# A ternary feed-forward split by batch, with keys loaded whole, in a gated cross-attention network

## The chip, the cores and the metric

One core of a Trainium2 chip runs the kernel. The metric is the device time of one execution in microseconds (us), the median of several runs. The engines are PE (matrix products; PEld is its weight load, which overlaps), DVE (vector), ACT (activation functions and copies), POOL and SP (which issues most DMAs). Each takes its instructions in order.

## The reference

Input x is 2 x 512 x 256 (1,024 tokens, 8 blocks of 128, four per batch), the context 2 x 1024 x 256. Four layers follow one another, each x = x + tanh(g) * attention(x, context) and then x = x + tanh(g) * ffn(norm(x)), with norms inside:

- layer 0: attention at sampled positions; an int8 feed-forward
- layer 1: attention with 16 heads of 8; a mixture of 8 experts (MoE), one expert per token, 192 tokens per expert at most
- layer 2: attention with 16 heads of 16; the ternary feed-forward
- layer 3: attention with 8 heads of 4; a channel-mixing feed-forward

The ternary feed-forward, with all weights in {-1, 0, 1} and a scale per output column, is

```
a  = silu((h @ w1) * s1) * ((h @ w2) * s2)     # 256 -> 1024, gated
b  = gelu((a @ h1) * t1)                       # 1024 -> 1024
c  = gelu((b @ h2) * t2)                       # 1024 -> 1024
y  = (c @ w3) * s3                             # 1024 -> 256
```

for every token by itself, so the two batches are independent in it. Softmax attention here subtracts the largest score of each row and head before the exponential.

## The kernel before

**Order of work.** The kernel is one program written layer by layer; a tile framework takes its instructions, gives them buffers by tags with a fixed number of slots, and orders the instructions of each engine by their dependences and slots. `keep_in_program_order` pins an instruction where it was written.

**Attention** (`attention`, from line 1042) works on the two batches in turn. `queries(b)` transposes the normalised blocks of batch b and multiplies with the query weights (L1070, L1076) into QT. Then, per block and group of heads, the scores of 128 queries are made (L1143, into `scores` or a bank) and their largest values reduced on DVE (L1150, L1152), which ends in qa. In the main part the scores are made again transposed (L1174), ACT takes the exponential (L1179), PE multiplies with the values (L1186). The first 20 largest-score steps, the lead, run before the first exponential; `queries(1)` goes beside them. What the layer in front still has to do is handed in as `before`: a function of a range of blocks that gives a generator of steps. It is called for batch 0's blocks ahead of everything; for batch 1's blocks its steps alternate with those of `queries(0)`, and what is left of them runs before the lead.

**Keys and values** of all attentions are computed at the start and kept in DRAM. K is stored per head in HD + 1 rows of 2,048 columns. `loaded_keys` (L1011 to L1026) makes one tile for four heads, each in a quarter of the 128 partitions: POOL sets the tile to zero (L1019), then one DMA per head brings its rows (L1021): 17 rows of 8 KB in layer 2, 5 in layer 3.

**MoE.** Each expert's products end in `ye`, stored to DRAM `yg`; its last part, `rest` (L1424 to L1438), gathers each block's rows with an indirect DMA on POOL (L1427) and adds them to x on DVE (L1434). It is the `before` of attention 2. The norm's statistics, square root (L161, ACT), reciprocal (L162, DVE) and offsets (L168) follow, and ACT makes h (L184).

**Ternary feed-forward** (`ternary_ffn`, from L1582). An fp32 activation is split in three bf16 parts (`split`, L1605 to L1608: two casts on ACT, two subtractions on DVE), each multiplied with the upper 16 bits of the weights, which are exact for ternary values. `upper` also reduces the lower 16 bits of every weight (L1596) into `low`. The norm of all eight blocks comes first, then the first layer over all 1,024 tokens; the second and third layer (`gelu_layer`) load a 512 KB slice of weights per 128 output columns (L1662, two slots) and multiply it with 1,024 tokens (L1634, 48 matmuls of 512 columns per slice). Then a matmul sums `low` (`psl`, L1683), `more` is read as a flag (L1685), and every engine branches over `any_weights` (L1689), a fallback for weights that are not ternary, which doesn't run with these inputs. w3T, attention 3's keys and values are loaded ahead of the flag. The last product (L1696) with the update of x (L1701, L217) is attention 3's `before`: eight blocks of 16 matmuls.

**The zeros** in DRAM that the MoE needs are written by `prepare_routing` beside attention 1, from a tile `zero`.

Of the kernel before, what the change touches and what calls it, by code (L numbers as in the profile page):

```python
# [8 lines left out]

# [70 lines left out]
class _Net:  # L80
# [829 lines left out]
    def prepare_context(self):  # L910
        nc = self.nc
        self.kd, self.vd = {}, {}
        for name, H, HD in (("l1", 16, 8), ("l2", 16, 16), ("l3", 8, 4)):
            k = self.dram.tile([H, HD + 1, B * M], F32, name=f"K_{name}")
            self.kd[name] = k
            nc.sync.dma_start(
                k[:, HD, :].rearrange("h (c m) -> h c m", m=P),
                _bc(self.ones[:H].unsqueeze(1), [H, B * M // P, P]),
            )
# [93 lines left out]
    def loaded_keys(self, name, H, HD):  # L1013
# [3 lines left out]
        for g in range(H // 4):  # L1017
            k = self.wide("KT")([P, B, M])
            nc.gpsimd.memset(k, 0.0)  # L1019
            for h in range(4):  # L1020
                nc.sync.dma_start(  # L1021
                    k[32 * h : 32 * h + HD + 1].rearrange("r b m -> r (b m)"),
                    self.kd[name][4 * g + h],
                )
            KT.append(k)
        return KT  # L1026

    def loaded_values(self, name, H):
        V = []
        for b in range(B):  # L1030
            v = self.big.tile([P, M // P, H * 32], F32, tag=f"v{b}", name=f"V{b}")
            self.nc.sync.dma_start(
                v, self.vd[name][ts(b, M)].rearrange("(j p) c -> p j c", p=P)
            )
            V.append(v)
        return V

    def attention(
        self, name, KT, V, H, HD, scale, gate, before, bq=None, bv=None, bo=None, aside=None
    ):  # L1040

# [50 lines left out]
        for _ in first:  # L1092
            next(second, None)
        for _ in second:
            pass
        second = queries(1)
# [149 lines left out]
        for k, _ in enumerate(up_to(LEAD, True)):  # L1246
            run_later()
            if k % 2:
# [51 lines left out]
    def moe_ffn(self, gate):  # L1300
# [121 lines left out]
        KT = self.loaded_keys("l2", 16, 16)  # L1422

        def rest(blocks, bank):  # L1424
            y = self.big.tile([P, BPB, D], F32, tag="e", name="yn", bufs=4)
            for k, n in enumerate(blocks):
# [5 lines left out]
                )  # L1432
            for k, n in enumerate(blocks):
                nc.vector.scalar_tensor_tensor(  # L1434
                    self.x[:, n, :], y[:, k, :], some[:, n : n + 1], self.x[:, n, :],
                    ALU.mult, ALU.add,
# [79 lines left out]
    def prepare_routing(self):  # L1516
# [6 lines left out]
        for to, k in ((self.xg[: NE * CAP], NE * CAP // P), (self.yg[NE * CAP :], T // P)):  # L1523
            nc.sync.dma_start(
                to.rearrange("(k p) f -> p k f", p=P), _bc(zero.unsqueeze(1), [P, k, D])
            )
        self.rank, self.first, self.behind = (
# [54 lines left out]
    def ternary_ffn(self, gate, loads):  # L1582
# [9 lines left out]
        def upper(w):  # L1592
# [6 lines left out]
            )  # L1599
            return w.bitcast(BF16).rearrange("p c (n two) -> p c n two", two=2)[:, :, :, 1]  # L1600
# [9 lines left out]
        hT = self.norm_transposed()  # L1610
        parts = self.big.tile([P, 3, DC, T], BF16, tag="v1", name="hTs")
        for n2 in range(NB // 2):
            at = ts(n2, 2 * P)
            r = self.big.tile([P, DC, 2 * P], F32, tag="avj", name="rest", bufs=2)
            split(hT[:, :, at], [parts[:, i, :, at] for i in range(3)], r)

        def stored(tags, name):

            tiles = []
            for i, part in enumerate(tags):  # L1620
                tiles.append([])
                for k, (tag, bufs, n) in enumerate(part):
                    t = self.big.tile([P, n, T], BF16, tag=tag, name=f"{name}{i}{k}", bufs=bufs)
                    tiles[-1] += [t[:, c] for c in range(n)]
            return lambda i, c, at: tiles[i][c][:, at]

        e2 = [("e", 4, HC // 2)] * 2
        h1 = stored((e2, e2, [("q", 1, HC)]), "hid1")

        def product(ps, w, oc, src, chunks):  # L1630
            for c in range(chunks):
                for i in range(3):
                    for t in range(2):
                        nc.tensor.matmul(  # L1634
                            ps[:, ts(t, 512)], lhsT=w[:, c, ts(oc, P)], rhs=src(i, c, ts_(t, 512)),
                            start=(c == 0 and i == 0), stop=(c == chunks - 1 and i == 2),
                        )

        def keep(dst, oc, at, make):
            g = self.big.tile([P, 512], F32, tag="avT", name="g", bufs=2)  # L1640
            make(g)
            r = self.big.tile([P, 512], F32, tag="avj", name="rest", bufs=2)
            split(g, [dst(i, oc, at) for i in range(3)], r)

        w1, w2 = upper(w12[:, 0]), upper(w12[:, 1])
        for oc in range(HC):
            pa = self.pss.tile([P, T], F32, tag="sc", name="pa")
            pb = self.pss.tile([P, T], F32, tag="sc", name="pb")
            for ps, w in ((pa, w1), (pb, w2)):
                product(ps, w, oc, lambda i, c, at: parts[:, i, c, at], DC)  # L1650
            si = self.wide("si")([P, T])
            nc.scalar.activation(si, pa, AF.Silu, scale=self.col("w1s")[:, oc : oc + 1])
            for t in range(2):
                at = ts_(t, 512)
                keep(h1, oc, at, lambda g: nc.vector.scalar_tensor_tensor(
                    g, pb[:, at], self.col("w2s")[:, oc : oc + 1], si[:, at], ALU.mult, ALU.mult,
                ))

        def gelu_layer(name, scale, src, done):
# [269 lines left out]
```

## Time and profile before

| what | us |
|---|---|
| median of 3 runs | 1298.85 (1297.12 to 1301.19) |
| profiled execution | 1298.23 |
| its span | 1296.5 |
| PE busy | 1156.7 (89%) |
| DVE busy | 720.3 (56%) |
| ACT busy | 607.5 (47%) |
| POOL busy | 228.3 (18%) |
| mean granted TensorE clock | 0.933 |

The span runs from the first to the last instruction; the execution's time is 1.7 us longer. Busy shares are means over stages with different limits, so the stages are to be looked at one by one. In order of time: the MoE's last product ends near 562, attention 2 has its first transposes at 587.3, its last product with the values near 844, the ternary first layer begins at 862.55 and ends at 909.3, the two wide layers end at 1075.3, the last product begins at 1084.1, attention 3's first exponential is at 1149.2, and the end is at 1296.5. In a timeline's line stand: start, duration, engine, line, operation, output<-inputs, shapes, count, and in brackets how long the engine had been idle and what ended it.

### The profile page before, as it was taken

The numbers are of one execution on the slowest core, as the hardware profiler recorded it, in microseconds if no ns is written. First come the engines' busy times: TensorE is split into PE (matmuls) and PEld (weight loads), VectorE is DVE, ScalarE is ACT, GpSimd is POOL, SyncE is SP. The second block draws the span as 40 slices with busy tenths as digits, with TensorE's granted clock in tenths as the row PEclk, the third lists the DMA queues.
The fourth block names the chain that finished last, engine by engine and source line by source line (L and its number), as shares of the span: only waits on it lengthen the run. The fifth ranks groups of instructions, "written<-read, shape, count | busy, mean of one in ns | idle before, by whom it ended". The sixth has DMA issues, their size and how long they took to land. (4 is left out here: it accounts for less than half of the span.)

```text
span 1296.5 us, 16857 instructions
## 1 busy us (share of the span) xinstructions
PE 1156.7 (89%) x6576; PEld 540.6 (42%) x6596; DVE 720.3 (56%) x1106; ACT 607.5 (47%) x1166; POOL 228.3 (18%) x204
## 2 busy tenths in 40 slices
PE   6987499999998989937999899969999997999977
PEld 3334333333334578823333233334444445543324
DVE  5794678787764111114788778448333111588635
ACT  2422236888874311103488678646333110258761
POOL 1043201334320200131033233000000000113200
PEclk9978698999999989977899999979999998989988
DMA  6033530000211345420000100000122112000000
GB/s 220 1 118 111 116 137 5 1 1 1 66 34 41 111 155 190 156 68 27 16 2 1 66 1 2 17 18 1 34 84 58 58 33 80 9 1 1 10 0 33
DMA packets 56837, 67.49 MB, mean 52 GB/s; under 512 B 4064, under 2 KB 45568, under 8 KB 56288
## 3 DMA queue, kind: packets, MB, share of 16 engines
q1 hardware_dynamic: 52856, 61.07, 15.0%
q0 software_dynamic: 896, 2.49, 0.7%
q10 hardware_dynamic: 2992, 2.70, 0.6%
q8 instruction: 57, 0.93, 0.3%
q14 instruction: 36, 0.29, 0.1%
HBM read 49.93 MB, written 16.32 MB: 51 GB/s over the span
## 5 line engine op out<-in xcount | busy, mean ns | idle before, releaser
L1152 DVE TENSOR_REDUCE part<-scores 128x2 f32<-128x1024 f32 x290 | 341.8, 1219 | 92.5 <-PE bank L1174 77.1
L1179 ACT ACTIVATE e<-bank 128x512 f32<-128x512 f32 x580 | 302.2, 601 | 121.1 <-PE bank L1174 89.4
L1174 PE MATMUL bank<-qa,KT 32*128 32x512 f32 x1160 | 306.1, 634 | 0.6 <-DVE o L1213 0.6
L1143 PE MATMUL scores<-KT,QT 32*128 32x512 f32 x1160 | 293.9, 641 | 4.2 <-DVE part L1152 4.2
L1198 POOL TENSOR_TENSOR avT<-avT,avj 128x512 f32<-128x512 f32 x113 | 143.2, 1268 | 345.9 <-ACT avj L1197 345.9
L1186 PE MATMUL bank<-e,V 128*32 128x512 f32 x1280 | 182.8, 607 | 2.5 <-ACT e L1179 2.5
L1143 PEld LDWEIGHTS scores<-KT,QT 32*128 32x128 f32 x1160 | 100.6, 190 | 157.3 <-DVE part L1152 115.3
L1634 PE MATMUL pg<-hid,wg_h 128*128 128x512 bf16 x752 | 165.1, 379 | 0.8
L1174 PEld LDWEIGHTS bank<-qa,KT 32*128 32x128 f32 x1160 | 117.2, 188 | 36.0 <-issue 18.2
L1634 PEld LDWEIGHTS <-wg_h 128*128 128x128 bf16 x768 | 75.1, 98 | 90.6
L1019 POOL MEMSET KT<- 128x2048 f32 x10 | 18.0, 1821 | 375.9 <-PE pg L1634 157.3
L1186 PEld LDWEIGHTS bank<-e,V 128*32 128x32 f32 x1280 | 28.3, 108 | 106.2 <-ACT e L1179 94.9
L1197 ACT COPY avj<-bank 128x512 f32<-128x512 f32 x113 | 69.2, 612 | 6.7 <-PE bank L1186 6.7
L1402 PE MATMUL py<-w2e,h 128*96 128x256 f32 x256 | 57.4, 379 | 0.0
L1596 DVE TENSOR_REDUCE low<-wg_h 128x1 f32<-128x1024 uint16 x16 | 19.5, 1217 | 57.1 <-DMA wg_h<-in_h2T 54.4
L1606 DVE TENSOR_TENSOR rest<-g,hid 128x512 f32<-128x512 f32 x32 | 21.2, 690 | 51.5 <-ACT hid L1605 51.3
L1070 PE MATMUL bank<-ident,h 128*128 128x128 f32 x48 | 11.7, 369 | 39.0 <-ACT h L184 32.2
L1402 PEld LDWEIGHTS py<-w2e,h 128*96 128x96 f32 x256 | 41.2, 163 | 12.2
L1386 PE MATMUL ph<-xeT,w1e 128*128 128x192 f32 x256 | 45.1, 337 | 0.0
L1386 PEld LDWEIGHTS ph<-xeT,w1e 128*128 128x128 f32 x256 | 43.6, 198 | 1.3 <-DVE xeT L109 0.6
L1076 PE MATMUL bank<-hT,w_l_wq 128*128 128x512 f32 x80 | 41.4, 644 | 2.1 <-DVE part L1150 1.4
L1667 ACT ACTIVATE hid<-pg,cols 128x512 f32<-128x512 f32 x16 | 10.1, 683 | 70.2 <-PE pg L1634 70.2
(303 smaller groups left out, 1325.2 us busy)
## 6 DMA issues: line engine op xcount, KB each, us to landing
w1e<-in_W SPq DMA_DIRECT2D x8, 1024.0 KB
w2e<-in_W SPq DMA_DIRECT2D x8, 1024.0 KB
V_l<-v1st SPq DMA_DIRECT2D x16, 256.0 KB
V<-V_l SPq DMA_DIRECT2D x2, 2048.0 KB
wg_h<-in_h1T SPq DMA_DIRECT2D x8, 512.0 KB
wg_h<-in_h2T SPq DMA_DIRECT2D x8, 512.0 KB
K_l<-kst SPq DMA_DIRECT2D x12, 256.0 KB
KT<-K_l SPq DMA_DIRECT2D x16, 136.0 KB
```

The source lines that it names most:

```text
L1076: nc.tensor.matmul(ps, lhsT=wq[:, dc, ts(c, P)], rhs=hT[:, dc, ts(b, S)], start=(dc == 0), stop=(dc == DC - 1),)
L1143: nc.tensor.matmul(sc[i], lhsT=QT[r : r + 32, g, (b * BPB + k) * P : (b * BPB + k + 1) * P], rhs=KT[g][r : r + 32, b, ts(half, 512)], star ...
L1152: nc.vector.tensor_reduce(to, both, AX.X, ALU.max, negate=True)
L1174: nc.tensor.matmul(t, lhsT=KT[g][r : r + 32, b, ts(j, P)], rhs=augmented[n][r : r + 32, :], start=True, stop=True,)
L1179: nc.scalar.activation(e[:, h, :], t, AF.Exp, scale=scale)
L1186: nc.tensor.matmul(po[32 * h : 32 * h + 32, :], lhsT=V[b][:, j, ts(4 * g + h, 32)], rhs=e[:, h, :], start=True, stop=True,)
L1197: nc.scalar.copy(t, po)
L1198: nc.gpsimd.tensor_tensor(part["oT"], part["oT"], t, ALU.add)
L1386: nc.tensor.matmul(ps[:, k // 2, k % 2, :CAP], lhsT=w1[:, dc, ts(4 * fp + k, P)], rhs=xeT[:, dc, :], start=(dc == 0), stop=(dc == DC - 1),)
L1402: nc.tensor.matmul(ps, lhsT=h1[:, fc, ts(t, HCAP)], rhs=w2[:, fc, :], start=(fc == 0), stop=(fc == HC - 1),)
L1606: nc.vector.tensor_tensor(r, g, hi, ALU.subtract)
L1634: nc.tensor.matmul(ps[:, ts(t, 512)], lhsT=w[:, c, ts(oc, P)], rhs=src(i, c, ts_(t, 512)), start=(c == 0 and i == 0), stop=(c == chunks - ...
```

## The change

1. K of layers 2 and 3 has 32 rows per head in DRAM. `prepare_routing` fills the unused rows with zeros, with three more DMAs on SP. `loaded_keys` brings a tile of four heads with one DMA of 128 rows of 8 KB (1 MB): four for layer 2, two for layer 3, with no memset. Layer 1 is as before.
2. In the MoE's `rest` the x updates of batch 1 are kept in program order.
3. The ternary feed-forward is computed batch by batch. Batch 0 is normalised first, its first layer begins, batch 1's norm goes beside it, then batch 1's first layer. Batch 0 goes through the second and third layer, with the check of the weights' lower bits (`note`) in that pass. Then come the flag and the branch, and only after them the loads of w3T, the keys, and the weights of the second layer again. Batch 0's last product (four blocks) lies beside the first four steps of batch 1's second layer. Batch 1's third layer and last product become attention 3's `before`.
4. `attention` has a new argument, `late`, set for attention 3 alone: `queries(0)` runs by itself, and every one of the 20 lead steps is followed by one step of a chain of batch 1's third layer (8 steps), its last product (4 steps) and `queries(1)`.
5. The gate of the feed-forward's update is now `own`: the gate, or zero where the fallback ran; the fallback does its own last product.

The core of the diff:

```diff
@@ attention K in DRAM
-            k = self.dram.tile([H, HD + 1, B * M], F32, name=f"K_{name}")
+            rows = HD + 1 if name == "l1" else 32
+            k = self.dram.tile([H, rows, B * M], F32, name=f"K_{name}")
...
@@ loaded_keys
-            nc.gpsimd.memset(k, 0.0)
-            for h in range(4):
-                nc.sync.dma_start(
-                    k[32 * h : 32 * h + HD + 1].rearrange("r b m -> r (b m)"),
-                    self.kd[name][4 * g + h],
-                )
+            kd = self.kd[name][4 * g : 4 * g + 4]
+            flat = k.rearrange("p b m -> p (b m)")
+            if kd.shape[1] == 32:
+                nc.sync.dma_start(flat, kd.rearrange("h r m -> (h r) m"))
+            else:
+                nc.gpsimd.memset(k, 0.0)
+                for h in range(4):
+                    nc.sync.dma_start(flat[32 * h : 32 * h + kd.shape[1]], kd[h])
...
@@ attention
         first, second = queries(0), before(range(BPB, NB), bank)
         for _ in first:
-            next(second, None)
-        for _ in second:
-            pass
-        second = queries(1)
+            if not late:
+                next(second, None)
+        if late:
+            second = chain(second, queries(1))
+        else:
+            for _ in second:
+                pass
+            second = queries(1)
...
         for k, _ in enumerate(up_to(LEAD, True)):
             run_later()
-            if k % 2:
+            if k % 2 or late:
                 next(second, None)
...
@@ MoE rest
+            stay = self.tc.keep_in_program_order if blocks.start else lambda i: i
             for k, n in enumerate(blocks):
-                nc.vector.scalar_tensor_tensor(
-                    self.x[:, n, :], y[:, k, :], some[:, n : n + 1], self.x[:, n, :],
-                    ALU.mult, ALU.add,
+                stay(
+                    nc.vector.scalar_tensor_tensor(
+                        self.x[:, n, :], y[:, k, :], some[:, n : n + 1], self.x[:, n, :],
+                        ALU.mult, ALU.add,
+                    )
                 )
...
@@ prepare_routing
+        for name, HD in (("l2", 16), ("l3", 4)):
+            for h in range(0, self.kd[name].shape[0], 8):
+                to = self.kd[name][h : h + 8, HD + 1 :, :]
+                nc.sync.dma_start(
+                    to.rearrange("h r m -> h (r m)").rearrange("h (c m) -> h c m", m=D),
+                    _bc(zero[:8].unsqueeze(1), [8, (31 - HD) * B * M // D, D]),
+                )
...
@@ ternary_ffn
+        def first_layer(b, dst):
+            for oc in range(HC):
+                ps = self.pss.tile([P, 2, S], F32, tag="sc", name="pab")
+                for k in range(2):
+                    product(ps[:, k], upper(w12[:, k]), oc, [parts[:, b, i] for i in range(3)], DC)
+                si = self.wide("si")([P, S])
+                nc.scalar.activation(
+                    si, ps[:, 0], AF.Silu, scale=self.col("w1s")[:, oc : oc + 1]
+                )
+                keep(dst, oc, lambda g: nc.vector.scalar_tensor_tensor(
+                    g, ps[:, 1], self.col("w2s")[:, oc : oc + 1], si, ALU.mult, ALU.mult
                 ))
+                yield
+        def layer(b, name, scale, src, done):
             for oc in range(HC):
                 w = self.big.tile([P, HC, P], F32, tag="o4", name="wg_h", bufs=2)
                 nc.sync.dma_start(w, d[name][:, ts(oc, P)].rearrange("(c p) n -> p c n", p=P))
+                if b == 0:
+                    note(w)
+                ps = self.pss.tile([P, S], F32, tag="sc", name="pg")
                 product(ps, upper(w), 0, src, HC)
+                done(oc, lambda g: nc.scalar.activation(
+                    g, ps, AF.Gelu, scale=self.col(scale)[:, oc : oc + 1]
+                ))
+                yield
...
+        normed(0)
+        note(w12[:, 0])
+        note(w12[:, 1])
...
+        steps = first_layer(0, h1[0])
+        for _ in range(2):
+            next(steps)
+        normed(1)
+        all_of(steps)
...
+        all_of(first_layer(1, h1[1]))
...
+        all_of(layer(0, "h1T", "h1s", h1[0], lambda oc, make: keep(to, oc, make)))
...
+        h3, steps = third(0, to)
+        all_of(steps)
...
-        w3 = self.weight("w3T", HID, D, self.big, "wide", bufs=4)
-        loaded = loads()
         flag = nc.values_load(more[0:1, 0:1], min_val=0, max_val=1)
         with self.tc.If(flag != 0):
-            self.any_weights(hT, h3)
+            self.any_weights(gate, hT)
+
+        w3 = self.weight("w3T", HID, D, self.big, "wide", bufs=4)
+        KT = keys()
+        V = [values(0)]
...
+        to1 = h2()
+        for oc, _ in enumerate(
+            layer(1, "h1T", "h1s", h1[1], lambda oc, make: keep(to1, oc, make))
+        ):
+            if oc < BPB:
+                last(h3, oc, self.ps1.tile([P, D], F32, tag="one", name="pw3"))
+        h31, steps1 = third(1, to1)
         def rest(blocks, bank):
+            if blocks.start == 0:
+                return
+            yield from steps1
+            V.append(values(1))
             for n in blocks:
-                ps = bank(D)
...
+                last(h31, n, bank(D))
                 yield
```

## The prediction

> **What bounds the kernel now.** I read the page's first two parts (share of each engine, the span in slices), then a table of busy time by stretches cut at the stages' borders, then the timeline at those borders, and last the transfers by tile. PE is the engine that ends things: 1156.7 of 1296.5 us. What can be won therefore lies where it stands still or runs at a low clock. The stretches (length; busy us of PE, PEld, DVE, ACT, POOL; granted clock; DMA share; GB/s):
>
> ```profile
> 562.00:587.30 25.30, 0.00 (x0) 0.00 (x0) 7.92 (x29) 2.13 (x4) 9.50 (x9) 0.60 0.21 68
> 862.50:868.00 5.50, 3.18 (x7) 1.01 (x8) 4.73 (x8) 3.54 (x7) 0.00 (x0) 0.50 0.00 0
> 868.00:909.30 41.30, 41.14 (x183) 18.34 (x184) 29.03 (x43) 25.43 (x37) 0.00 (x0) 0.96 0.00 1
> 909.30:1075.30 166.00, 165.16 (x755) 75.43 (x769) 41.84 (x54) 40.71 (x67) 3.61 (x2) 1.00 0.18 53
> 1075.30:1084.00 8.70, 0.09 (x1) 0.00 (x1) 0.16 (x1) 2.55 (x3) 0.00 (x0) 0.73 0.90 243
> 1084.00:1090.30 6.30, 6.21 (x17) 5.00 (x18) 0.00 (x0) 0.00 (x0) 0.00 (x0) 0.56 0.17 49
> 1090.30:1117.00 26.70, 26.70 (x125) 22.74 (x124) 11.14 (x31) 4.24 (x8) 0.00 (x0) 1.00 0.00 1
> 1119.00:1149.20 30.20, 26.74 (x113) 11.92 (x117) 25.69 (x37) 6.71 (x12) 5.62 (x3) 0.80 0.02 6
> ```
>
> Row 1: 25.3 us without a matmul between the MoE layer and attention 2. Rows 2 and 3: the ternary first layer starts in gaps. Row 4: its two 1024-wide layers leave PE no gap, and DVE is idle three quarters of the time. Row 5: at the flag PE stands for 8.7 us, with the DMA engines 0.90 busy. Row 6: the first block of the last product at half clock. Row 8: attention 3's lead (20 largest-score steps before its first exponential) holds DVE for 25.69 of 30.2 us. So: DVE is idle beside PE's longest stretch, and PE then waits for DVE.
>
> **Keys as whole loads, and the pinned updates.** Inside row 1 (start, us, idle before and releaser):
>
> ```profile
> 569.92 1.05 POOL L1427 DMA_INDIRECT yn<-yg,gt  x1 [6.07 <-DMA KT<-K_l]
> 575.67 0.48 DVE L1434 SCALAR_TENSOR_TENSOR x<-yn,gt,x 128x256 f32<-128x256 f32 x1 [13.23 <-DMA yn<-yg,gt]
> ...
> 582.52 0.20 ACT L161 ACTIVATE rs<-rs 128x4 f32<-128x4 f32 x1 [18.42 <-DVE rs L160]
> 583.53 0.48 DVE L1434 SCALAR_TENSOR_TENSOR x<-yn,gt,x 128x256 f32<-128x256 f32 x1 [1.05 <-DMA yn<-yg,gt]
> 584.81 0.48 DVE L1434 SCALAR_TENSOR_TENSOR x<-yn,gt,x 128x256 f32<-128x256 f32 x1 [0.79 <-DMA yn<-yg,gt]
> ...
> 586.26 0.16 DVE L162 RECIPROCAL rs<-rs 128x4 f32<-128x4 f32 x1
> ...
> 587.30 0.29 PEld L1070 LDWEIGHTS bank<-ident,h 128*128 128x128 f32 x2 [25.75 <-ACT h L184]
> ```
>
> The 16 loads of 17 rows move 26 to 28 GB/s at a DMA share of 0.06, one engine of 16; the gathers, behind the last memset (562.05 to 563.85), begin at 569.92. In the change four loads of 1 MB take the place of 16 of 136 KB, and at the 214 to 347 GB/s that the 512 KB weight loads show they are over in 3 to 5 us each, before or while the last product runs. The gathers wait for the last store of `yg` (issued 562.48) alone: they begin between 564 and 570, I take 567, -3. Their landing time of 5.6 to 6.0 us stays, +-1.
>
> The pin: the square root was done at 582.72, but its reciprocal ran at 586.26, behind batch 1's updates and statistics, which waited for later gathers. In the changed program's order on DVE, rs, reciprocal and nb of batch 0 stand ahead of all four updates of batch 1. The chain starts 586.26-582.72 = 3.5 us earlier. Batch 1's norm is then late by nothing that counts: PE has batch 0's transposes and queries first. Together -6.5, about -7 with the memsets gone; ends -2 (the last whole load meets store and gathers) and -11.
>
> What pays: zeros for the extra rows, 2 x 0.98 MB and 1.77 MB written during attention 1, three issues on SP. Cover: the DMA engines move 1 to 5 GB/s there (7th to 10th of the page's 40 slices). If uncovered 3.7 MB at 200 to 350 GB/s are 11 to 19 us, but of DMA, not of PE; I take 0.
>
> **Ternary start, batch by batch.** Now 853.4 (statistics of all eight blocks) to the first matmul at 862.55, and gaps until 868: 46.8 us to 909.3 for 192 matmuls of 0.216 (the layers' mean below) = 41.5. In the change batch 0 is normalised inside attention 2's last steps; its split needs attention 2's V1 tile, free with the last values matmul (844.3). ACT pays there: two table loads of 1.28, rs 0.2, two h of 0.6, 4.0 us in a stretch where four exponentials of 0.54 fill the 2.1 us step; attention 2's end is 0 to 4 us later (857 instead of 853). Batch 0 is then missing only four transposes, copies and the split, some 5 us behind: first matmul about 858 to 860, with 2 to 3 us of gaps. Half-width products make ACT nearly co-bound in batch 0 (three operations of about 0.6 per column block, 14.4 us, and batch 1's norm and split, some 6, against 20.7 of PE). I take the end 3 us earlier, ends -8 and +4.
>
> **Layers 2 and 3.** 166 us before are 768 matmuls, so 0.216 each; there are as many matmuls after. New is that every weight is loaded twice, 32 loads instead of 16, each lasting PE only 24 x 0.216 = 5.2 us instead of 10.4, with two buffers. A load starts when the weight two before it is done with. The row for its length:
>
> ```profile
> 1002.78 0.37 SPq L1662 DMA_DIRECT2D wg_h<-in_h2T  x1
> 1006.64 1.22 DVE L1596 TENSOR_REDUCE low<-wg_h 128x1 f32<-128x1024 uint16 x1 [8.14 <-DMA wg_h<-in_h2T]
> ```
>
> 3.86 us from issue to use: 1.3 us to spare, cost 0. The Trainium skill speaks against it ("DMA: Bandwidth & Descriptors", Bandwidth, and Latency and other measured facts): 64 KB in 0.95 us and 1 MB in 6.15, thus an estimated 3.4 for 512 KB, and about 2 us of fixed cost, 5.4 in all. By that each of some 30 loads would stall PE 0.2 us, +6. The row is this very load, so I take 0 and keep +6 for the range.
>
> **Flag and last product.** What PE does there:
>
> ```profile
> L1689 PEldq COMPARE_BRANCH  x1: 7700/7700/7700, 1076.1 to 1076.1; - x1
> 1084.09 21.04 PE L1696 MATMUL bank<-w_w3T,hid 128*128 128x256 f32 x84 [8.71 <-PEq L1689]
> ```
>
> Its branch took 7.7 us while two V loads of 2 MB ran; at the kernel's first flag PE's branch took 3.56 us with a gap of 3.8, at the MoE's 4.7. After the change no such load is in flight, but w3T (1 MB) is now issued behind the branch: about 1.1 (flag to SP) + 0.6 + 1 + 3 = 5.7, plus start of PE. Between 4 and 9 I take 6.5, -2. The next weight stands on SP behind w3T and two key loads, 3.5 MB, lands some 13 us after the flag, while two blocks of last product (6.2 cold, 3.5) cover 6.5 + 9.7 = 16 us: hidden, with 3 us to spare. The clock: row 6 shows 6.3 us for a block that later takes 3.45, 2.85 lost. The skill ("TensorE: Matmul & The Clock Gate", Part 1) has half rate after an idle window of about 3.4 us and until about 3.4 us of work, 1.7 lost; by both a gap of 6.5 still pays, so I keep 2.8 and credit nothing, though a shorter gap looks as if it should.
>
> **Attention 3's lead.** Before, from 1084.1 to the first exponential at 1149.16: 65.1 us (27.6 last product, cold start, queries(0) in its gaps, 30.2 lead). The matmuls don't change, their neighbours do. From the end of the first layer:
> - before: 166 + 8.7 + 65.1 = 239.8.
> - after: batch 0's layers 83; flag 6.5; batch 0's last product 13.8 + 2.8; batch 1's second layer 41.5; queries(0) alone, where PE goes back and forth with ACT and DVE copies, 7 (before it was woven into the last product and cost 4 to 5); eight third-layer steps of 5.2 with two score matmuls between (0.37 each and a slot change, 0.9) 48.5; batch 1's last product with scores 13.8 + 3.6; then statistics, transposes and queries(1) with the eight largest left of 20, at 1.2 to 1.5 of DVE each, 11. Sum 231.5.
>
> So -8. Score and layer tiles take turns in two PSUM slots: a layer's slot is freed by a 0.68 us GELU during the 0.8 us of scores, a score slot by a 1.2 us reduce during 5.2 us of layer; no wait is left. Named costs: ACT's table reloads, 1.28 each, lie under matmuls of batch 1's second layer; ends of this part -16 (lead to 6, queries(0) at no cost) and +8 (bubbles of queries(0) cold, twelve instead of eight largest after).
>
> Sum: -7 - 3 - 8 = -18 on the profiled 1298.2 us (span 1296.5 and 1.7 around it), thus 1280.2; the median shown is 0.6 above that execution: 1281.
>
> **Rivals.**
> 1. Slower: weight reloads become the bound. Place: batch 0's and 1's layers; 32 loads, 5.2 us each. For: nothing shows two loads in flight with keys, w3T and values, and slack is 1.3. Against: DMA share 0.18 now, 0.36 doubled. Price: each us over 5.2 costs 32; the 18 us won are gone at a period of 5.75. At 6.0 (0.8 x 32 = 26) the time is 1307.
> 2. Part of it only: one of the three gains fails (gathers held up by a whole load; or attention 2's tail pays the full 4; or queries(0) and the exposed w3T eat the lead). For: all sit in chains through four engines. -8: 1291.
> 3. More: gathers at 565, flag gap 4, lead tail 6: -28, 1271. For: DVE has 124 idle us beside the layers.
> 4. The change doesn't do what it says: scores placed in the third layer still wait for PE's order and DVE stays the bound of the lead. The order of instructions speaks against it; it would give 1288 to 1298, no more than the first two gains or none.
>
> **How the numbers follow.** A measurement of this kernel tells 0.3% (3.9 us) from nothing. Likeliest case 0.50 (1281, own range 1274 to 1289); rival 2 0.19 (1286 to 1297); rival 3 0.08; rival 4 0.06, a third of it within 3.9 us; rival 1 0.17, mostly slower, a little of it within. Faster 0.79, same 0.06, slower 0.15. The range leaves out half of rival 1 and of rival 3: 1269 to 1304.
>
> **What would show it.** Right: PE idle before attention 2 18 us instead of 25; reciprocal directly behind the square root; wg_h loads landing under 4.5 us and PE without gaps in 32 layer steps; PE's gap at the flag 5 to 8; largest reduces between the third layer's steps, and 11 to 14 us from batch 1's last x update to the first exponential (31 before). Wrong: PE waiting for wg_h, a wait of a layer tile for a reduce, a clock under 0.9 in queries(0), or attention 2's end over 4 us late.

## The result, and the profile after

Forecast: 1281 us (range 1269 to 1304), faster with a chance of 0.79. Measured: 1305.04 us, median of 17 runs, beside 1298.66 us of the kernel before, median of 17. The ratio is 1.0047 (95% interval 1.0028 to 1.0065): the change makes the kernel about 6 us slower. The forecast is wrong in sign, and the time lies just over the range.

The profiled execution took 1305.04 us with a span of 1303.1. Here is the table of busy time by stretches of the kernel after, cut at its own borders (columns as before: length; busy us of PE, PEld, DVE, ACT, POOL; granted clock; DMA share; GB/s):

```profile
569.60:585.80 16.20, 0.01 (x1) 0.01 (x1) 5.33 (x18) 2.15 (x4) 7.69 (x8) 0.66 0.41 127
858.30:903.40 45.10, 43.72 (x197) 20.11 (x201) 34.20 (x53) 33.46 (x56) 0.00 (x0) 0.97 0.00 1
903.40:986.30 82.90, 82.48 (x378) 37.66 (x384) 31.29 (x36) 23.92 (x37) 0.00 (x0) 1.00 0.35 102
986.30:996.90 10.60, 0.09 (x2) 0.06 (x1) 0.28 (x2) 0.67 (x1) 0.00 (x0) 0.73 0.49 165
996.90:1054.30 57.40, 57.14 (x251) 32.47 (x257) 16.00 (x33) 17.31 (x26) 0.00 (x0) 0.96 0.36 108
1054.30:1063.10 8.80, 6.93 (x24) 2.83 (x22) 1.72 (x3) 5.13 (x9) 3.27 (x2) 1.00 0.20 60
1063.10:1112.90 49.80, 49.44 (x219) 20.29 (x222) 10.05 (x12) 4.81 (x7) 0.00 (x0) 1.00 0.22 64
1112.90:1131.70 18.80, 18.80 (x85) 12.99 (x84) 9.08 (x18) 1.97 (x2) 0.00 (x0) 1.00 0.21 70
1131.70:1154.80 23.10, 20.81 (x62) 7.44 (x63) 11.72 (x21) 6.13 (x11) 2.35 (x1) 0.78 0.05 12
```

Row by row: the stretch without a matmul ahead of attention 2; the first layer; batch 0's two wide layers; the flag; batch 0's last product with batch 1's second layer; `queries(0)`; batch 1's third layer with largest scores; batch 1's last product; the end of the lead, up to the first exponential. What the reader is to see: largest-score steps now lie beside batch 1's third layer and last product, as was meant (12 of the 20), and yet 23.1 us follow the last product in which PE is busy at a clock of 0.78 and DVE only half of the time.

Stage by stage, after minus before, in us. The second profile of the kernel after is experiment 8.

| stage | before | after | second profile | difference | forecast |
|---|---|---|---|---|---|
| up to the MoE's last product | 562.0 | 569.6 | 566.0 | +7.6, +4.0 | 0 |
| to attention 2's first transpose | 25.3 | 16.2 | 16.1 | -9.1 | -7 |
| attention 2 and the first layer | 322.2 | 317.6 | 317.9 | -4.6, -4.3 | -3 |
| end of first layer to first exponential | 239.7 | 251.4 | 254.7 | +11.8, +15.1 | -8 |
| to the end | 147.3 | 148.4 | 148.4 | +1.1 | 0 |

Two of the three gains came, the third turned into a loss of 12 to 15 us. The first row is dealt with in experiments 8 and 9.

Ahead of attention 2 (timeline of the kernel after: start, us, idle before and releaser):

```profile
575.75 1.04 POOL L1435 DMA_INDIRECT yn<-yg,gt  x1 [119.17 <-DMA yg<-ye]
578.56 0.48 DVE L1445 SCALAR_TENSOR_TENSOR x<-yn,gt,x 128x256 f32<-128x256 f32 x1 [8.53 <-DMA yn<-yg,gt]
...
584.49 0.20 ACT L162 ACTIVATE rs<-rs 128x4 f32<-128x4 f32 x1 [12.81 <-DVE rs L161]
584.73 0.18 DVE L163 RECIPROCAL rs<-rs 128x4 f32<-128x4 f32 x1 [0.27 <-ACT rs L162]
...
585.79 0.29 PEld L1074 LDWEIGHTS bank<-ident,h 128*128 128x128 f32 x2 [16.65 <-ACT h L185]
```

The gather starts when the last store lands, 6.2 us after the last product (before: 7.9), its rows are used 2.8 us later (before: 5.8), and the reciprocal follows the square root directly.

The flag, and then the lead's end:

```profile
990.71 0.40 SPq L121 DMA_DIRECT2D w_w3T<-in_w3T  x1
...
996.87 8.50 PE L1742 MATMUL pw<-w_w3T,hid 128*128 128x256 f32 x28 [10.51 <-DMA w_w3T<-in_w3T]
```

```profile
1136.09 1.79 ACT L185 ACTIVATE h<-x,nb,rs 128x256 f32<-128x256 f32 x3 [2.24 <-DVE nb L169]
...
1142.80 0.18 DVE L1165 TENSOR_TENSOR nms<-part 128x16 f32<-128x16 f32 x1
...
1144.59 5.45 PE L1080 MATMUL bank<-hT,w_l_wq 128*128 128x512 f32 x8
...
1151.03 0.66 PE L1170 MATMUL bank<-ident,nms 128*128 128x128 f32 x4
...
1154.78 1.19 ACT L1187 ACTIVATE e<-bank 128x512 f32<-128x512 f32 x2 [2.71 <-PE bank L1182]
```

A group of heads needs 16 largest-score steps. The last four steps of batch 0's first group are among the eight that are left here; with them its largest values are complete at 1142.80 (`nms`). Their transposes, which the first exponential needs, run only at 1151.03, 8 us later: in PE's order they stand behind batch 1's queries (L1080). And the granted clock is low there:

```profile
1140.00:1145.00 5.00, 5.00 (x8) 1.66 (x8) 1.33 (x4) 0.58 (x1) 1.27 (x1) 0.50 0.02 3
1145.00:1150.00 5.00, 5.00 (x10) 1.70 (x9) 0.92 (x1) 0.69 (x1) 0.00 (x0) 0.69 0.00 0
```

### The profile page after: what moved, and what is told of

Its sections match the earlier page's. It is cut to its first block, busy times and chain, and to the rows that moved or that the text cites. A ratio compares the mean times of both kernels' runs of the same rounds, so it can differ in the third digit from the quotient of the medians.

```text
span 1303.1 us, 16834 instructions
## 1 busy us (share of the span) xinstructions
PE 1169.5 (90%) x6574; PEld 541.1 (42%) x6596; DVE 721.9 (55%) x1110; ACT 617.3 (47%) x1179; POOL 217.2 (17%) x198
## 5 line engine op out<-in xcount | busy, mean ns | idle before, releaser
L1644 PE MATMUL pg<-hid,wg_h 128*128 128x512 bf16 x501 | 139.9, 379 | 0.6
L1158 DVE TENSOR_REDUCE part<-bank 128x1 f32<-128x512 f32 x60 | 38.0, 683 | 27.7 <-PE bank L1151 27.0
L1644 PE MATMUL pg<-hid2l,wg_h 128*128 128x512 bf16 x124 | 47.0, 379 | 0.1
L1080 PE MATMUL bank<-hT,w_l_wq 128*128 128x512 f32 x80 | 44.4, 689 | 2.9 <-ACT hT L1075 2.3
L1644 PE MATMUL pab<-hTs,w 128*128 128x512 bf16 x188 | 42.9, 384 | 3.4 <-ACT hTs L1630 2.2
```

The lines of the kernel that those rows point to most:

```text
L1080: nc.tensor.matmul(ps, lhsT=wq[:, dc, ts(c, P)], rhs=hT[:, dc, ts(b, S)], start=(dc == 0), stop=(dc == DC - 1),)
L1158: nc.vector.tensor_reduce(to[:, i : i + 1], sc[i], AX.X, ALU.max, negate=True)
L1644: nc.tensor.matmul(ps, lhsT=w[:, c, ts(oc, P)], rhs=src[i][:, c, :], start=(c == 0 and i == 0), stop=(c == chunks - 1 and i == 2),)
```

## The experiments

All ratios are to the kernel before, measured beside it. A difference of 0.001 is 1.3 us.

**1. Keys and pin alone.** The kernel before with parts 1 and 2 of the change.

```diff
+            rows = HD + 1 if name == "l1" else 32
+            k = self.dram.tile([H, rows, B * M], F32, name=f"K_{name}")
...
+                nc.sync.dma_start(flat, kd.rearrange("h r m -> (h r) m"))
...
+            stay = self.tc.keep_in_program_order if blocks.start else lambda i: i
```

> The kernel before with parts 1 and 2 alone (keys of 32 rows and whole loads, zeros, pinned updates of batch 1). Theory: these win the 9.1 us that PE waits less ahead of attention 2 (25.3 to 16.2 in the two profiles), nothing else moves: 1290 us, ratio 0.993. Rival: the new layout of the keys in DRAM makes the first 180 us of the kernel slower, as the profile after shows them (its zero tile is set at 185.7 instead of 178.2, in a stretch whose instructions are the same): then about 1298 and the zero tile near 186 again, and the gain is eaten there.

Measured: 1291.27 us, ratio 0.9954 (0.9938 to 0.9971), a gain of 6 us. PE's wait ahead of attention 2 is 16.2 us, the same as in the kernel after:

```profile
577.04 1.18 PE L1073 MATMUL bank<-ident,h 128*128 128x128 f32 x4 [16.19 <-ACT h L184]
```

The time from the first layer's end to the first exponential is also 3.5 us shorter (236.1 for 239.7), 1.1 of it at the flag. The measured gain is smaller than these stages add up to; experiment 9 looks into that. The zero tile came at 180.0, neither as before nor as in the first profile after.

**2. The ternary part alone.** The changed kernel with the old keys and without the pin.

```diff
-                nc.sync.dma_start(flat, kd.rearrange("h r m -> (h r) m"))
+                self.nc.sync.dma_start(flat[32 * h : 32 * h + kd.shape[1]], kd[h])
...
-            stay = self.tc.keep_in_program_order if blocks.start else lambda i: i
```

> The changed kernel without parts 1 and 2: old keys with memsets, no pin, the ternary layers batch by batch. Theory: the ternary part by itself loses 8 us (first layer 4 earlier, then 20 lost at flag, lead and lead's end against the 8 forecast won): 1307 to 1313, ratio 1.006 to 1.011. Rival (early part slower by the layout): old layout, zero tile near 178, and 1305 or less.

Measured: 1317.57 us, ratio 1.0161 (1.0122 to 1.0200): 21 us slower than before, about twice what was expected. Put on top of experiment 1, the same part costs 0.0093, 12 us. So keys and pin are worth 15 us in this order, not 6. In the profiles 9.3 of them lie ahead of attention 2 (PE waits 25.6 us there instead of 16.2), and 7 between the flag and the end of the last product (152.4 for 145.4). Behind the flag the eight loads of attention 3's keys (timeline of this kernel: SP, then PE)

```profile
993.91 5.53 SPq L1024 DMA_DIRECT2D KT<-K_l  x8
1000.44 1.22 SPq L1661 DMA_DIRECT2D wg_h<-in_h1T  x2
...
1018.64 0.93 PE L1070 MATMUL bank<-ident,h 128*128 128x128 f32 x4 [3.20 <-ACT h L185]
...
1027.64 0.38 PE L1629 MATMUL pg<-hid,wg_h 128*128 128x512 bf16 x1
```

keep the second layer's weights on SP until 1000.44, 12.5 us after the sum of `low` (in the kernel after 993.40, 7.0 after it). PE's order differs too: it does all four blocks of batch 0's last product and `queries(0)`, with a wait of 3.2 us, and begins batch 1's second layer at 1027.64 (in the kernel after 1005.42, between two blocks). That the late weights made the scheduler choose this order is likely, and not shown.

**3. Batch 1's queries out of the lead.** The changed kernel; the transposes and query products of batch 1 go beside batch 0's exponentials, only their statistics stay.

```diff
-            if k % 2 or late:
+            if late and k < 13 or not late and k % 2:
                 next(second, None)
-        for _ in second:
-            pass
+        if not late:
+            for _ in second:
+                pass
...
                         exponentials(n, j, e, {h: bank(S) for h in ((0, 1) if half else (2, 3))})
+                        if late and n == 0 and second is not None:
+                            if next(second, self) is self:
+                                self.add_bias(bias, 1)
+                                second = None
```

> The changed kernel with the transposes and query products of batch 1 taken out of the lead and done beside batch 0's exponentials; its statistics stay in the lead. Theory: the lead's end (1131.7, last matmul of the last product, to 1154.8, first exponential: 23 us, forecast 11) is long because batch 1's norm, transposes and queries stand in PE's order between the scores and the transposes of the largest values, and PE goes cold there. Without them it is 11 to 15 us, about 5 us come back in the main part: 1297 to 1301, ratio to the kernel before 0.998 to 1.002. Rival: DVE's eight largest steps set the lead's end by themselves; then it stays over 19 us and the time at 1304 to 1308.

Measured: 1299.28 us, ratio 1.0006 (0.9985 to 1.0027), 5 us less than the kernel after. The lead's end:

```profile
1131.90:1144.80 12.90, 10.16 (x44) 4.04 (x44) 12.36 (x22) 2.58 (x4) 0.00 (x0) 0.74 0.07 22
```

It falls from 23.0 to 12.9 us, DVE is now busy for 12.36 of them, and from the first exponential to the end it takes 154.8 instead of 148.4. The transposes of the largest values now follow them at once, where they came 8 us behind:

```profile
1138.55 0.19 DVE L1165 TENSOR_TENSOR nms<-part 128x16 f32<-128x16 f32 x1
...
1138.79 1.12 PE L1170 MATMUL bank<-ident,nms 128*128 128x128 f32 x4 [1.55 <-DVE nms L1165]
```

The theory holds: 10 of the 23 us are batch 1's transposes and queries, which stood ahead in PE's order; in the other 13 DVE is busy with the eight largest steps that were left. 6.4 of the 10 come back later. The run takes away the work together with its place: no run only moved the transposes of the largest values ahead of the queries.

**4. w3T and keys ahead of the flag, no fallback.** The fallback for weights that aren't ternary is replaced by one gated zero in the branch that isn't taken, so this kernel is right for ternary weights only.

```diff
+        w3 = self.weight("w3T", HID, D, self.big, "wide", bufs=4)
+        KT = keys()
         flag = nc.values_load(more[0:1, 0:1], min_val=0, max_val=1)
         with self.tc.If(flag != 0):
-            self.any_weights(gate, hT)
-
-        w3 = self.weight("w3T", HID, D, self.big, "wide", bufs=4)
-        KT = keys()
+            self.nothing(gate)
```

> The changed kernel with w3T and attention 3's keys loaded ahead of the flag; the fallback for weights that aren't ternary is left out, which makes room for them (it doesn't run with these inputs). Theory: PE's gap at the flag, 10.6 us, is 3.8 of branch, some 2.7 of SP's way through it and 6.1 of w3T's load; with the load ahead it is 4 to 5.5, a gain of 5 to 6 and of a part of the cold matmuls behind it: 1298 to 1300, ratio to before 0.999 to 1.002. Rival: the gap is the branch and what PE's sequencer fetches behind it, and stays over 8: time unchanged at 1305.

Measured: 1289.57 us, ratio 0.9947 (0.9926 to 0.9967): 13 us less than the kernel after, more than twice what was expected. There is no gap at the flag at all: PE goes from the sum of `low` to batch 1's second layer in 0.1 us, at a clock of 1.00. The scheduler now issues the first two weights of that layer ahead of the flag too, since nothing in the branch needs their buffers. Which of the three (loads, weights, branch) did it, this run cannot tell.

**5. No fallback, nothing else moved.**

> The changed kernel with the fallback for weights that aren't ternary left out and nothing else moved: w3T and the keys are loaded behind the flag in the program. It asks what made the earlier run without the fallback gain 15 us, when its profile has no gap at the flag (PE's branch 0.23 us instead of 3.84): the loads ahead or the short branch. Theory (the branch's time is that of what lies behind it; the loads count too): branch 0.2 to 0.5 us, gap 0 to 8 depending on whether the loads stay behind it, 1292 to 1300. Rival (the loads are all): branch near 3.8 and time 1303 to 1306.

Measured: 1290.16 us, ratio 0.9961 (0.9941 to 0.9981). The branch, and PE's stretch around it (line, form and shortest, median and longest duration in ns; then the busy table):

```profile
L1733 PEldq COMPARE_BRANCH  x1: 235/235/235, 981.7 to 981.7; - x1
```

```profile
981.00:997.00 16.00, 15.95 (x75) 9.77 (x75) 3.88 (x9) 3.90 (x6) 0.00 (x0) 1.00 0.28 81
```

Written behind the flag, the loads again went ahead of it when the fallback was gone (w3T was issued at 903.6, PE's branch is at 981.7). So experiments 4 and 5 are one: without the fallback's code PE's branch is 0.23 us instead of 3.84 and nothing holds the loads back, 11 to 13 us by the ratios. Early loads and short branch are not told apart by these two; experiment 6 has the early loads alone.

**6. w3T and keys ahead of the flag, fallback kept.** The loads are moved as in experiment 4, and the fallback's buffers have other tags.

```diff
-        f1, f2, f3 = (self.wide(f"f{i}")([P, HC, N]) for i in range(3))
+        f12 = self.big.tile([P, 2, HC, N], F32, tag="v0", name="f12")
+        f1, f2 = f12[:, 0], f12[:, 1]
+        f3 = self.big.tile([P, HC, N], F32, tag="e", name="f3", bufs=4)
```

> The changed kernel, complete with its fallback, with w3T and attention 3's keys loaded ahead of the flag (the fallback's buffers moved to other tags; V of batch 0 is loaded behind the flag instead). Theory: the branch stays at 3.6 to 4.0 us, the 6.1 us of w3T leave the gap (10.6 to about 4.5), cold matmuls stay: 6 less than the changed kernel, 1297 to 1300, ratio to before 0.998 to 1.001. Rival: V's 2 MB behind the flag delay the second layer's weights of batch 1 and PE waits there instead: 1303 to 1306.

Measured: 1299.86 us, ratio 1.0028 (1.0009 to 1.0047). The gap:

```profile
985.33 4.95 PE L1742 MATMUL pw<-w_w3T,hid 128*128 128x256 f32 x14 [4.60 <-PEq L1735]
```

It is 4.6 us, and what ends it is the branch (3.56) and no longer the load: as the theory has it. From the sum of `low` to the first exponential it takes 164.6 instead of 168.4 us, 3.8 less, where the gap alone is 5.9 shorter: the rest is lost again on the way, 1.0 of it at the lead's end (24.0 for 23.0). The rival's wait for weights behind V's 2 MB did not come. By the ratios the gain is 2.5 us, under the 6 expected, and the intervals of this run and the kernel after overlap.

**7. Experiments 6 and 3 together.**

> The kernel of the run with early w3T and fallback, and batch 1's transposes and query products beside batch 0's exponentials. Theory: both gains add, 6 and 6, as they lie in different stages: 1290 to 1295, ratio 0.993 to 0.998, faster than both kernels. Rival: one eats the other, 1297 or more.

Measured: 1291.40 us, ratio 0.9965 (0.9943 to 0.9988). The two add: 0.0082 less than the kernel after, 10.6 us; alone they gave 0.0019 and 0.0041, and the difference to their sum is within the noise. This kernel, which has its fallback, is faster than the kernel before.

**8. The changed kernel again,** for a second profile.

> The changed kernel again, for a second profile. Theory: the zero tile's time (185.7 in the first profile, 178.2 before) is chance of the granted clock in the first stage and will differ by some us from profile to profile; the stages from the MoE's end on agree with the first profile within 2 us each. Rival: it is fixed by the new layout of the keys and is again at 185 to 186.

Measured: 1305.02 us, one run. The zero tile is at 182.4 this time, 185.7 in the first profile. The two profiles agree ahead of attention 2 (16.1 and 16.2) and in its length within 0.3 us; between the flag and the first exponential they differ by 3.3, more than the 2 expected (1.6 of it at the flag: 12.1 for 10.5).

**9. The layout of the keys alone.** 32 rows per head in DRAM, no zeros written, old loads, no pin.

```diff
+            rows = HD + 1 if name == "l1" else 32
+            k = self.dram.tile([H, rows, B * M], F32, name=f"K_{name}")
...
-                    self.kd[name][4 * g + h],
+                    self.kd[name][4 * g + h, : HD + 1],
```

> The kernel before with 32 rows per head in DRAM for the keys of layers 2 and 3, and nothing else: no zeros are written, the loads are the old ones of 17 and 5 rows with memsets, the updates aren't pinned. The run of keys and pin gained 6 us (ratio 0.9954), while its stages add up to 12. Theory: the rest is chance of the clock in single profiles, the layout costs nothing: ratio 0.998 to 1.002. Rival: the wider pitch slows the stores of the keys and the first stage, 3 to 6 us: ratio 1.002 to 1.005, and the zero tile's time 181 or later.

Measured: 1296.25 us, ratio 0.9996 (0.9975 to 1.0017), zero tile at 180.5. The layout costs nothing that can be told (the interval allows 3 us either way). In the fourteen profiles of this study the zero tile came between 177.5 and 185.7, with the same instructions ahead of it, and the runs of one kernel scatter by 2 to 5 us (standard deviation) along with their mean granted clock: in the 22 runs of experiment 1 time and clock correlate with -0.91, about 1.1 us for 0.001 of clock. A single profile is no measure of a few us in the first stage.

**10. The pin alone.**

> The kernel before with the updates of batch 1 kept in program order (part 2 alone). Theory: reciprocal and offsets of batch 0 come 3.5 us earlier, PE waits 22 instead of 25.3 us ahead of attention 2: 1293 to 1295, ratio 0.997. Rival: the gathers that the key loads slow hold batch 0 as well, the pin alone gains under 1 us: ratio 0.999 to 1.001.

Measured: 1293.46 us, ratio 0.9966 (0.9951 to 0.9981), a gain of 4.4 us. The reciprocal follows the square root, and PE waits 21.4 instead of 25.3 us:

```profile
581.88 0.18 DVE L162 RECIPROCAL rs<-rs 128x4 f32<-128x4 f32 x1 [0.27 <-ACT rs L161]
...
582.94 1.18 PE L1070 MATMUL bank<-ident,h 128*128 128x128 f32 x4 [21.42 <-ACT h L184]
```

3.5 were forecast for this step: right. The rest of the 9.1 (5.2) is the whole loads'.

**11. Keys and pin, values behind the flag.** Experiment 1 with attention 3's two loads of 2 MB issued behind the flag.

```diff
-        loaded = loads()
+        KT, values = loads()
         flag = nc.values_load(more[0:1, 0:1], min_val=0, max_val=1)
         with self.tc.If(flag != 0):
             self.any_weights(hT, h3)
+
+        loaded = KT, values()
...
-        f1 = self.wide("f1")([P, HC, N])
+        f1 = self.big.tile([P, HC, N], F32, tag="v0", name="f1")
```

> The kernel before with parts 1 and 2, and the values of attention 3 (two loads of 2 MB) issued behind the flag instead of ahead of it; the fallback's two buffers have other tags for this. It asks what makes PE's branch 7.7 us before and 6.6 with keys and pin, but 3.4 to 3.8 where no large load runs beside it. Theory: the loads slow what PE fetches at the branch; with them behind it the branch is 3.3 to 4 and the gap 4.5 instead of 7.6: 3 us less than keys and pin, 1287 to 1289, ratio 0.991 to 0.994. Rival: the branch's time doesn't hang on the loads: it stays over 6 us, ratio 0.995 to 0.997.

Measured: 1286.35 us, ratio 0.9919 (0.9892 to 0.9945), the lowest here, with its fallback and without any splitting of the ternary layers.

```profile
L1703 PEldq COMPARE_BRANCH  x1: 4520/4520/4520, 1072.4 to 1072.4; - x1
```

PE's branch falls from 6.62 (experiment 1) to 4.52 us and its gap from 7.6 to 5.5: the loads in flight do lengthen it. The DMA share during PE's branch was 0.94 in experiment 1, 0.22 here, and 0.05 in the kernel after, with its 3.84. The gap explains 2.1 us of the 4.5 between the ratios of the two runs; their intervals overlap, so the size of this gain is less sure than its direction.

**12. Two largest steps per step of batch 1's third layer,** on top of experiment 7, and one per block of its last product: none is left for the lead's end.

```diff
-            if late and k < 13 or not late and k % 2:
+            if late and (k % 2 or k >= 16) or not late and k % 2:
                 next(second, None)
+        if late:
+            next(second, None)
...
-                largest(ahead, lead and ahead // 2 % 2 == 1)
+                largest(ahead, lead and ahead // (1 if late else 2) % 2 == 1)
```

> The kernel of the run with early w3T and later queries, and now two largest-score steps beside each step of batch 1's third layer and one beside each block of its last product, so that none of the 20 is left behind the last product (in that run 8 are, and 12.5 us lie between the last product and the first exponential). Theory: batch 0's exponentials follow the last product directly, 1 to 4 us; the eight steps moved forward cost PE about 1 us each there (6.4 to 7.4 per third-layer step), so the net gain is 1 to 5: 1286 to 1290, ratio 0.991 to 0.996. If this holds, the split pays only with all of this, and then no more than keys, pin and later values give without any split (0.9919). Rival: score tiles and layer tiles, now three in two slots, make PE wait for DVE: third-layer steps over 8 us and 1292 or more.

Measured: 1290.11 us, ratio 0.9943 (0.9925 to 0.9961). The first exponential comes 3.4 us after the last product, as the theory has it, but neither theory had this (timeline between two steps of the third layer):

```profile
1073.93 0.70 PE L1151 MATMUL scores<-KT,QT 32*128 32x512 f32 x2
...
1073.94 0.70 PE L1151 MATMUL bank<-KT,QT 32*128 32x512 f32 x2
```

The score matmuls of the two largest steps use different rows of the array, start 10 ns apart and run beside each other. A third-layer step is 6.36 us with two of them and 6.35 with one: the second was free. The rest went elsewhere. From the sum of `low` to the first exponential it takes 143.6 us (experiment 7: 153.1), and then 157.8 to the end (154.1; kernel after: 148.4), with a granted clock of 0.71 in the first 17.6 us (0.85 in experiment 7, 1.00 in the kernel after). Against experiment 7 the gain is 0.0022, within both intervals.

## Why the prediction was wrong

**Keys and pin: right, in part by luck.** -7 was forecast, -9.1 came (experiments 1 and 10): 3.9 in PE's wait from the pin, and 5.2 from the loads. Of these 1.7 is the earlier start of the gathers, for which 3 was taken; the larger part is a term that the sum held constant, the gathers' landing, 2.8 us instead of 5.8. One term too large and one left out made up for each other. The zeros are hidden: from the zero tile to the MoE's first product 282.4 us before and 282.7 after.

**First layer: right.** -3 was forecast; -4.6 in the two profiles that were compared. Over all runs, five profiles with the old order lie between 318.7 and 323.6 us for attention 2 and first layer, nine with the new one between 317.6 and 322.6: the size isn't sure, the sign is likely.

**Layers 2 and 3: right, and the reloaded weights did not become the bound, as rival 1 feared.** Batch 0's two layers take 83.0 us for the 83 forecast, at a clock of 1.00. The weight's row in the kernel after,

```profile
980.20 1.22 DVE L1618 TENSOR_REDUCE low<-wg_h 128x1 f32<-128x1024 uint16 x1 [4.14 <-DMA wg_h<-in_h2T]
```

belongs to a load issued at 975.9: 4.3 us, inside the 5.2 that a weight lasts. The trace's 3.86 was the better guide than the 5.4 estimated from the Trainium skill ("DMA: Bandwidth & Descriptors", Bandwidth, and Latency and other measured facts), which would have stalled PE.

**Flag: mis-sized.** The term was "about 1.1 (flag to SP) + 0.6 + 1 + 3 = 5.7", and 6.5 in all. PE's own branch was as forecast (3.84), but SP issued w3T 4.3 us after the sum of `low` (986.36 to 990.71), not 1.1, and the load took 6.1, not 4.6: a gap of 10.5, and 12.1 in the second profile. SP's own branch took 0.05 us (at 987.1), but the next instructions recorded for SP on that line, eight semaphores, came only 2.7 us later. The profile before had the same kind of row, 6.7 us behind SP's branch at 1076.1, and the 1.1 overlooked it (line, form, durations in ns, first and last start in us; before, then after):

```profile
L1689 SPq EVENT_SEMAPHORE  x8: 17/17/17, 1082.8 to 1085.4; - x8
L1733 SPq EVENT_SEMAPHORE  x8: 17/17/17, 989.8 to 990.3; - x8
```

Experiment 6 takes the load away and leaves 4.6. Moving the loads behind the branch cost more than leaving V in flight beside it had. `queries(0)` (8.8 for 7) and the third layer with the last product behind it (68.6 for 65.9) add some 4 us.

**Lead's end: the step that failed.** It was "statistics, transposes and queries(1) with the eight largest left of 20, at 1.2 to 1.5 of DVE each, 11". That is DVE's work alone; the two parts were taken as lying beside each other. They lie one after the other: PE works in order, batch 1's transposes wait for the norm, the scores of the steps left stand between them, `nms` waits for the first four of the eight, and its transposes wait behind batch 1's queries. Meanwhile the granted clock fell to 0.50. It took 23.1 us instead of 11, 12 of the 20 that the sum is off from the first layer's end to the first exponential (251.4 for 231.5). How much of the 12 is the order and how much the low clock isn't separated; PE's 20.8 busy us at a mean of 0.78 would be an estimated 16 at 1.00. Experiment 3 takes the queries out: 12.9. Experiment 12 also takes the eight largest out: 3.4. Before, these 20 steps were 30.2 us with 25.69 of DVE; the forecast saw that DVE would be relieved, and not that a chain of other engines stood close behind it.

**Where the expected gain went.** The largest scores did go under the third layer; what they freed is given back at the flag and at the lead's end. Even with both mended (experiment 12: 143.6 us from the sum of `low` to the first exponential, with one batch's two layers, 83 us, in it), part comes back in attention 3's main part, 157.8 for 147.3 to the end. Experiment 11 has the lower median with no split.

**What stays open.** Added up over the last four rows of the table, the kernel after is within 1 us of the kernel before in its first profile and 2.6 longer in its second, while the medians differ by 6. The difference lies in the first stage (+7.6 and +4.0). So of the first profile's miss the steps above account for 17 us, from the -18 forecast for these four rows to the -0.8 that came; what is left is the first stage's. The layout isn't its cause (experiment 9), the instructions there are the same, and chance of the clock is of that size in single profiles; whether it would leave a mean over 17 runs isn't shown. In the same way experiment 1's stages add up to more than its 6 us. Why the main part after an early first exponential is slower by 6 to 10 us was seen only as a low clock, not tested.

## What to carry to other kernels

When work is moved off the engine that bounds a stretch, write down the chain that starts it and ends it in each engine's own order: here the stretch went from 30 us bound by DVE to 23 us set by the order of PE's queue, where batch 1's queries, which nothing needed yet, stood ahead of the transposes that the first exponential waited for. A load that is moved behind a branch costs the issuing engine's way through the branch and its own time to land, so what the next stage needs at once is best in before the flag (experiment 6), and large loads that it doesn't need yet are best issued behind it (experiment 11). The small parts of a change can be worth more than its large one: three edits to loads and order (experiment 11) win 0.8%, and the restructuring around them loses what they give.

## What the runs showed of the hardware

- The branch over the ternary fallback, untaken, took PE 0.23 us when that code was a few instructions. Over the whole fallback it took 3.3 to 3.9 us at a DMA share of 0.04 to 0.05, 4.5 at 0.22 (experiment 11), and 6.6 to 7.7 with 4 MB of loads in flight (share 0.91 to 0.95: the kernel before, experiments 1, 9 and 10). ACT, POOL, DVE and SP took 0.05 to 0.06 us at the same branch, but over the whole fallback SP's next instruction came 2.7 to 6.7 us later.
- Loads of 17 rows ran at a DMA share of 0.06 to 0.07 and 27 to 28 GB/s, as one busy engine of 16 would give. Gathers beside them landed in 5.6 to 6.7 us (the kernel before, experiments 9 and 10); with whole loads instead they landed in 2.7 to 2.8 (experiments 8 and 11).
- Four score matmuls of 32 rows each, in different rows of the array, took the time of two (experiment 12: third-layer steps of 6.36 us with four, 6.35 with two in the kernel after).
- Runs of one kernel (11 runs or more) spread over 9 to 18 us and go with the mean granted clock, 0.7 to 1.5 us for 0.001; a stage of equal instructions ended at 177.5 in one profile and at 185.7 in another.
